# A graph attention layer pair: the edge counts as an added logarithm instead of a multiplication

## The chip, the cores and the metric

The kernel runs on one core of a Trainium2 chip. The metric is the device time of one execution in microseconds (us). The engines named below are TensorE (PE, with PEld for its weight loads), VectorE (DVE), ScalarE (ACT), GpSimd (POOL) and SyncE (SP, which issues most DMAs). Each engine works through its own queue in order; semaphores hold one back for another.

## The reference

Two graph attention layers over 512 nodes and 16,896 directed edges (8192 drawn pairs in both directions, and one loop per node), a residual and a layer norm. The first layer has 8 heads of 768 features, the second one head.

```python
def gat_layer(x, W, a_s, a_d, b, edge_index, concat):
    h = (x @ W).reshape(n, H, C)
    alpha_s = jnp.einsum('nhc,hc->nh', h, a_s)
    alpha_d = jnp.einsum('nhc,hc->nh', h, a_d)
    e = jax.nn.leaky_relu(alpha_s[src] + alpha_d[dst], NEG_SLOPE)
    m = jax.ops.segment_max(e, dst, num_segments=n)
    e = jnp.exp(e - m[dst])
    denom = jax.ops.segment_sum(e, dst, num_segments=n)
    alpha = e / (denom[dst] + EPS)
    msg = h[src] * alpha[:, :, None]
    out = jax.ops.segment_sum(msg, dst, num_segments=n)
    return out.reshape(n, H * C) + b
...
h = jax.nn.elu(gat_layer(x, W1, a_src1, a_dst1, b1, edge_index, concat=True))
x = _layernorm(x + gat_layer(h, W2, a_src2, a_dst2, b2, edge_index, concat=True))
```

An edge that occurs k times counts k times in the sum and in the denominator, and once in the maximum.

## The kernel before, in words

The edges are turned into a dense 512 by 512 matrix of counts, `cnt` (float32, four row blocks of 128 nodes, `[128, 4, 512]`), and a mask `absent` (bfloat16) that is 0 where there is an edge and 1e30 where there is none (`counted`, L490). Softmax is then done on dense rows. For a head h and a row block t:

- `lift` (L569, ACT) makes the negated logits of the block, 128 x 512, in a tile `q`;
- `leak` (L575, DVE) applies the leaky slope;
- `rank` (L578) adds the mask and takes the row minimum in one DVE instruction (L581, followed by a short read of the accumulator into `nmax`), and then ACT takes the exponential (L583);
- `weigh` (L788, DVE) multiplies by the counts and sums the row in one instruction (L791, followed by a read of the accumulator), adds a small constant (L794) and takes the reciprocal (L795);
- `turn_out` and `turn_in` (L809, L818) scale the block on ACT (L811), take it apart into halves of 16 bits (L814), transpose it by a DMA (L816), and put it back into `PT` (L819).

The whole order is written out by hand (`manual_schedule`); no scheduler moves anything. All products of matrices are of the Strassen kind: fewer products, more sums and differences on DVE, which are put between the matmuls as "fill". Head 0's first projection and the counting of edges come first (to about 60 us). Then, for each head h from 0 to 6, the loop at L991 has three stages:

- `mixed` (L869): the aggregation of head h, 256-column matmuls of L891, with the ELU on ACT and DVE;
- `second` (L442): this head's share of the second layer's projection, seven products P1, P2, P6, P7, P4, P5, P3, each for i = 0 and 1, matmuls of L364 with 384 columns. Their results are emptied from PSUM by ACT (L455) or DVE (L457, L459). **P4 is accumulated on the bank of P7, and P3 on that of P5**, after DVE has read the bank: so P4 waits for the emptying of P7. The loop at L1032 (n = 2 to 6) issues one product pair per step and puts between them, for head h + 1, `leak` and `rank` of block n - 2, `lift` of block n - 1, the emptying of the first half (`e0`), for n > 3 `weigh` and `turn_out` of block n - 4, and the emptying of the second half (`e1`);
- the projection of head h + 2 (`projection`, L382, or from head 3 on `by_thirds`, L407, matmuls of L423).

Head 0's own softmax runs earlier, with `rank` at L735 and `weigh` in `give` (L954), beside the counting and the projection of head 1. The second layer's aggregation and the layer norm (L1234 on) end the kernel.

In the trace each matmul of L364 stands as two instructions, so a step n of `second` (two products of three matmuls) has 12.

The program has a second copy of the whole pass, for edge lists that the first can't count; it is not run with these inputs. The lines that set the order in `second` are these:

```python
q = [lift(h + 1, 0)]
for n in range(2, 7):
    (m0, e0), (m1, e1) = pairs[2 * n:2 * n + 2]
    m0()
    if not last:
        m1()
    if n < 6:
        leak(q[n - 2])
        rank(q[n - 2], n - 2)
    if n < 5:
        q.append(lift(h + 1, n - 1))
    ...
    e0()
```

Of the kernel before, what the change touches and what calls it, by code (L numbers as in the profile page):

```python
# [8 lines left out]
F32 = mybir.dt.float32  # L9
# [4 lines left out]
AF = mybir.ActivationFunctionType  # L14
ALU = mybir.AluOpType
# [3 lines left out]
EPS_DEN = 1e-16  # L19
EPS_LN = 1e-5  # L20
NO_EDGE = -1e30


def kernel(tc: tile.TileContext, *args):
# [12 lines left out]
def gat_pass(  # L37
# [16 lines left out]
    nc = tc.nc  # L54
    P = 128
# [15 lines left out]
    const = ctx.enter_context(tc.tile_pool(name="const", bufs=1))  # L71
# [3 lines left out]
    small = ctx.enter_context(tc.tile_pool(name="small", bufs=4))  # L75
# [171 lines left out]
    for j in range(2):  # L247
        nc.vector.tensor_reduce(picks[:, j:j + 1], ident.rearrange("p (j k) -> p k j", k=32)[:, j, :], axis=AX.X,
                                op=ALU.add)
    far = const.tile([P, 1], F32, name="far")  # L250
    nc.vector.memset(far, -NO_EDGE)
    wide = keep.tile([P, 2, SQ], F32, name="wide")
    nc.vector.memset(wide, 0.0)

# [69 lines left out]
    cnt = keep.tile([P, NT, N], F32, name="cnt")  # L324
    absent = keep.tile([P, NT, N], BF16, name="absent")
# [243 lines left out]
    def lift(h, t):  # L569

        q = BC[h] if 0 < h < H and t + 1 == NT else qpool.tile([P, N], F32, name="q")
        nc.scalar.activation(q, BC[h][:, :N], AF.Identity, bias=AL[h][1][:, t:t + 1], scale=-1.0)
        return q
# [4 lines left out]
    def rank(q, t):  # L578

        nmax = small.tile([P, 1], F32, name="nmax")  # L580
        nc.vector.tensor_tensor_reduce(out=q, in0=q, in1=absent[:, t, :], scale=1.0, scalar=-NO_EDGE,  # L581
                                       op0=ALU.add, op1=ALU.min, accum_out=nmax)
        nc.scalar.activation(q, q, AF.Exp, bias=nmax, scale=-1.0)  # L583
        return q

    def turn_b1():
        psb = mm.tile([P, 512], F32, name="mm")
# [12 lines left out]
    if not general:  # L600
# [95 lines left out]
        for n, batch in enumerate(batches):  # L696
# [32 lines left out]
            if n + 1 == len(batches):  # L729
                spread(0)  # L730
                q = [lift(0, t) for t in range(NT)]
# [11 lines left out]
    else:  # L743
        for t in range(NT):
            ps = mm.tile([P, 512], F32, name="mm")
            for c in range(EC):
# [3 lines left out]
                                        op0=ALU.is_equal)  # L750
# [36 lines left out]

    def weigh(q, t, scale=True):  # L788

        den = small.tile([P, 1], F32, name="den")  # L790
        nc.vector.scalar_tensor_tensor(q, q, 1.0, cnt[:, t, :], op0=ALU.mult, op1=ALU.mult,  # L791
                                       accum_out=den)
        rden = small.tile([P, 1], F32, name="rden")
        nc.vector.tensor_scalar(rden, den, EPS_DEN, None, op0=ALU.add)  # L794
        nc.vector.reciprocal(rden, rden)  # L795
        if scale:
            nc.vector.tensor_scalar(q, q, rden, None, op0=ALU.mult)  # L797
        return rden
# [192 lines left out]
    for h in range(H - 1):  # L991
        if 0 < h < H - 2:
            B3, rest_of_thirds = load_thirds(h + 2)
        elif h:
            A[H] = []
            for j, a in ((2, a_src2[0]), (4, a_dst2[0])):
                v = wpool.tile([P, HK, HALF], F32, name=f"w2t{j}").rearrange("p k n -> p (k n)")[:, :D]
                nc.sync.dma_start(v, row_bcast(a))
                A[H].append(v)
            last_sum = load_w2(H - 1, "w2")  # L1000
        GA, gsums = left(gT, gS)
        halves = [half_logits(h + 1, t) for t in ((0, 1) if h else (0, 1, 3))]
        besides[2:2] = [s_ for s_, _ in halves] + [lambda: row_out(h + 1)]
        finish = mixed(h, AA, BB, besides + [d_ for _, d_ in halves] + behind)
        besides, behind = [], []
        if h == 0:
            load_w1(2)()
        if h + 2 < H:
            load_a(h + 2, a_src1[h + 2], a_dst1[h + 2])
            attend = attended(h)  # L1010
        pairs = second(h, GA, B2)
        for m, _ in pairs[:2]:
            m()
        pairs[0][1]()
        for f in finish:
            f()
        gsums[0]()
        pairs[1][1]()
        gsums[1]()
        if pending:  # L1020
            pending.pop(0)()
        pairs[2][0]()
        gsums[2]()
        pairs[3][0]()
        gsums[3]()
        if pending:
            pending.pop(0)()
        pairs[2][1]()
        pairs[3][1]()
        last = h + 2 == H  # L1030
        q = [lift(h + 1, 0)]
        for n in range(2, 7):  # L1032
            (m0, e0), (m1, e1) = pairs[2 * n:2 * n + 2]
# [4 lines that stand above are left out]
                leak(q[n - 2])  # L1038
                rank(q[n - 2], n - 2)
            if n < 5:  # L1040
                q.append(lift(h + 1, n - 1))
            if last:

                if n > 4:
                    turn_in(n - 5)
                if n == 6:
                    turn(q[2], 2)
                if n == 6:
                    weigh(q[3], 3)
                m1(lambda: turn(q[3], 3) if n == 6 else None)  # L1050
            if not last and n == 6:
                turn_in(0)
                turn_out(q[2], 2, weigh(q[2], 2, scale=False))
            e0()
            if last and 2 < n < 6:
                weigh(q[n - 3], n - 3)
                if n < 5:
                    turn_out(q[n - 3], n - 3)
            if not last and 3 < n < 6:
                turn_out(q[n - 4], n - 4, weigh(q[n - 4], n - 4, scale=False))  # L1060
            if not last and n == 6:
                turn_out(q[3], 3, weigh(q[3], 3, scale=False))
                if 0 < h:
                    sums = rest_of_thirds()
                    reload_x()
                load_w2(h + 1)()
            e1()
            for f in in_second[:1]:
                f()
            del in_second[:1]  # L1070
            if 0 < h and not last and 2 < n < 6:
                attend[n - 3]()
        if 0 < h and h + 2 < H:
            pairs = by_thirds(h + 2, XB, B3)
            AA, sums3 = left_sums(h + 1)
            B2, sums2 = right(W2[h + 1], "w1")
            for n in range(15):
                pairs[n][0]()
                for p in {0: ("P6", "P2"), 1: ("P4",), 4: ("P10",), 5: ("P0",), 6: ("P1",), 9: ("P7",),
                          12: ("P3",)}.get(n, ()):  # L1080
                    sums[p]()
                if n == 5:
                    BB, rsums_ = right_sums()
                    sums3 += rsums_
                if n in (2, 3, 5, 6, 8, 9, 10):
                    for _ in range(2 if n == 8 else 1):
                        sums3.pop(0)()
                if n in (11, 13):
                    logits(h + 2, HS[h + 2], 2 + (n - 11) // 2)
                if n in in_third:  # L1090
                    in_third.pop(n)()
                if n == 14:
                    sums2[0]()
                    behind = sums2[1:]
                pairs[n][1]()
                if n in (1, 2, 4):
                    turn_in((n + 2) // 2)
            assert not sums3
        elif h + 2 < H:
            B_, sums = right(W1[h + 2], "w2")  # L1100
            pairs = projection(h + 2, XA, B_)
            for n in range(14):
                pairs[n][0]()
                if n == 0:
                    for f in attend:
                        f()
                    B2, sums2 = right(W2[h + 1], "w1")
                if n in (1, 3):
                    sums[n // 2]()
                if n == 1:  # L1110
                    AA, sums3 = left_sums(h + 1)
                pairs[n][1]()
                if n in (1, 2, 4):
                    turn_in((n + 2) // 2)
                if n == 5:
                    BB, sums3 = right_sums()
                if 1 <= n < 9:
                    sums3.pop(0)()
                if n == 0:
                    XB, early, store, late_ = x_thirds()  # L1120
                if n in (2, 3, 5, 6, 7, 8, 9):
                    early.pop(0)()
                if n == 9:
                    store()
                if n in (10, 12):
                    logits(h + 2, HS[h + 2], 2 + (n - 10) // 2)
                if n == 13:
                    late_["P10"]()
                    behind = [sums2[0], late_["P8"]]
                    in_second, in_third = [sums2[1], late_["P13"], late_["P9"]], {2: late_["P12"], 7: late_["P5"]}  # L1130
        else:
            last_sum()
            B2, sums2 = right(W2[H - 1], "w1")
# [65 lines left out]
    q, rden = [lift(H, 0)], []  # L1199
# [96 lines left out]
```

## Time and profile before

| what | us |
| --- | --- |
| median of three runs (641.05 to 641.44) | 641.15 |
| the profiled execution's own time | 640.93 |
| its span, first to last instruction | 639.1 |
| PE busy | 628.2 |
| DVE busy | 525.8 |
| ACT busy | 305.9 |
| mean granted clock of TensorE | 0.998 |
| L791 on DVE, 36 times, without the reads of its accumulator | 24.6 |
| reads of that accumulator, 36 times | 3.0 |
| L583 on ACT, 36 times | 25.8 |
| table loads on ACT, 2 | 1.3 each |

"Busy" is the union of an engine's instructions. Matmuls overlap each other in the records, so a short stop between two of them does not show as idle time; it shows in the distance between their starts. The timeline gives starts and durations in us, neighbouring instructions of one kind in one row (x12: twelve of them), and in brackets how long the engine had been idle before, and for whom it waited.

### The profile page before, as it was taken

To read this page: it belongs to the slowest core of one execution; us is meant where nothing else is said; L and a number is where in the kernel's file an instruction comes from. 1 tells how busy PE (TensorE), PEld (TensorE's weight loads), DVE (VectorE), ACT (ScalarE), POOL (GpSimd) and SP (SyncE) were. 2 spreads that over 40 slices of the span, in tenths; PEclk is the share of its full clock that TensorE was granted. 3 is DMA by queue.
4 is the path that set the end of the run, shared out by engine and by line. 5 is a ranking of instruction groups with operands and counts; after the bars stand their busy time and mean duration, and the time that the engine had idled before them with its cause. 6 is when DMAs were issued, how large, how long until landed. Compare 5 with 4: busy or idle time off the path is not lost.

```text
span 639.1 us, 7665 instructions
## 1 busy us (share of the span) xinstructions
PE 628.2 (98%) x2509; PEld 435.4 (68%) x2509; DVE 525.8 (82%) x1138; ACT 305.9 (48%) x510; POOL 63.6 (10%) x105
## 2 busy tenths in 40 slices
PE   8999999999999999999999999999999999999995
PEld 5555586556756886588857886588857886645553
DVE  8989889897789878878788878878888878876775
ACT  5874745730718145551728145551728145543440
POOL 1300011010300220010300230010300110000000
PEclk9999999999999999999999999999999999999999
DMA  8993488696905987099925986198915991410122
GB/s 299 325 237 90 89 237 276 156 265 213 261 23 89 325 228 185 17 269 235 235 73 109 316 228 174 21 269 240 237 59 125 318 303 23 116 40 1 31 60 77
DMA packets 86844, 109.87 MB, mean 172 GB/s; under 512 B 40150, under 2 KB 67982, under 8 KB 86030
## 3 DMA queue, kind: packets, MB, share of 16 engines
q1 hardware_dynamic: 70590, 87.42, 42.6%
q0 software_dynamic: 15776, 21.30, 19.9%
q10 hardware_dynamic: 432, 0.59, 0.3%
q8 instruction: 22, 0.36, 0.2%
q14 instruction: 24, 0.20, 0.1%
HBM read 95.12 MB, written 2.90 MB: 153 GB/s over the span
## 4 chain that ended last, share of the span: by engine, by line
PE 94%; DVE 3%; DMA 1%; ACT 1%; issue 0%; SPq 0%; POOL 0%; DVEq 0%; POOLq 0%; ACTq 0%
PE mm L364 43%; PE mm L423 20%; PE mm L891 18%; PE mm L837 3%; PE mm L1242 3%; PE held L364 2%; PE tr L664 1%; DMA a_s<-in_L_gnn_a_src_dram 1%; PE held L544 1%; PE bc L664 0%; ACT os L636 0%; DVE offsets L309 0%; PE tr L1166 0%; DMA drow<-turned 0%; DVE h L459 0%
## 5 line engine op out<-in xcount | busy, mean ns | idle before, releaser
L364 PE MATMUL mm<-w,gT 128*128 128x384 f32 x252 | 83.6, 486 | 0.0
L583 ACT ACTIVATE q<-q,nmax 128x512 f32<-128x512 f32 x36 | 25.8, 721 | 92.4 <-DVE nmax L581 92.4
L364 PEld LDWEIGHTS mm<-w,gT 128*128 128x128 f32 x252 | 47.9, 190 | 31.9
L891 PE MATMUL mm<-PT,hs 128*128 128x256 f32 x252 | 61.3, 379 | 0.0
L364 PE MATMUL mm<-w1t,gS 128*128 128x384 f32 x180 | 60.6, 487 | 0.0
L429 ACT ACTIVATE hs<-mm 128x512 f32<-128x512 f32 x30 | 17.9, 596 | 87.0 <-PE mm L423 72.4
L891 PEld LDWEIGHTS mm<-PT,hs 128*128 128x128 f32 x252 | 47.8, 190 | 7.3 <-issue 0.4
L364 PEld LDWEIGHTS mm<-w1t,gS 128*128 128x128 f32 x180 | 34.1, 190 | 24.0 <-DVE w1t L356 0.5
L431 DVE TENSOR_TENSOR hs<-hs,mm 128x512 f32<-128x512 f32 x45 | 30.8, 685 | 23.0 <-PE mm L423 21.8
L459 DVE TENSOR_TENSOR h<-h,mm 128x384 f32<-128x384 f32 x72 | 38.9, 547 | 12.6 <-PE mm L364 12.3
L891 PE MATMUL mm<-pS,gS 128*128 128x256 f32 x168 | 43.2, 380 | 0.0
L819 ACT COPY PT<-zr 128x1024 uint16<-128x1024 uint16 x34 | 39.3, 1156 | 2.6 <-DMA zr<-pS 1.9
L423 PE MATMUL mm<-w2r,xT 128*128 128x256 f32 x160 | 37.9, 380 | 0.0
L423 PE MATMUL mm<-w2r,gT 128*128 128x256 f32 x160 | 37.5, 382 | 0.0
L891 PEld LDWEIGHTS mm<-pS,gS 128*128 128x128 f32 x168 | 31.8, 190 | 4.7 <-DVE pS L864 0.4
L423 PEld LDWEIGHTS mm<-w2r,xT 128*128 128x128 f32 x160 | 30.3, 190 | 5.4 <-DVE hs L431 0.2
L423 PEld LDWEIGHTS mm<-w2r,gT 128*128 128x128 f32 x160 | 30.0, 190 | 5.8 <-DVE hs L431 1.9
L364 PE MATMUL mm<-w1t,gT 128*128 128x384 f32 x96 | 32.4, 487 | 0.0
L895 ACT COPY u<-mm 128x256 f32<-128x256 f32 x21 | 7.8, 372 | 48.7 <-PE mm L891 48.7
L638 DVE TENSOR_SCALAR os<-nodes,idx 128x512 bf16<-128x512 f16 x104 | 29.5, 358 | 1.4 <-PE tr L664 1.4
L814 ACT COPY pS<-q 128x1024 uint16<-128x1024 uint16 x26 | 27.1, 1044 | 4.2 <-DVE q L797 3.6
L364 PE MATMUL mm<-w,gS 128*128 128x384 f32 x84 | 28.7, 487 | 0.4 <-DVE h L459 0.4
(233 smaller groups left out, 1264.8 us busy)
## 6 DMA issues: line engine op xcount, KB each, us to landing
w2r<-in_L_gnn_W_dram SPq DMA_DIRECT2D x48, 384.0 KB, 10.3
w<-in_L_gnn_W_dram SPq DMA_DIRECT2D x43, 384.0 KB, 10.6
gT<-xd SPq DMA_DIRECT2D x5, 1280.0 KB
w1t<-in_L_gnn_W_dram SPq DMA_DIRECT2D x9, 576.0 KB
w<-in_L_gnn_W_dram POOLq DMA_DIRECT2D x8, 576.0 KB, 8.5
w1t<-in_L_gnn_W_dram POOLq DMA_DIRECT2D x7, 576.0 KB, 9.6
w2t<-in_L_gnn_W_dram SPq DMA_DIRECT2D x15, 256.0 KB, 6.9
w2t<-in_L_gnn_W_dram POOLq DMA_DIRECT2D x15, 256.0 KB, 8.9
```

Of the source, the lines that this page charges most:

```text
L364: nc.tensor.matmul(ps[:, :HALF], A_[p][:, k, i * P:(i + 1) * P], B_[p][:, k, :], start=start and k == 0, stop=k == HK - 1, skip_group_chec ...
L423: nc.tensor.matmul(bank[chain][:, i * TH:(i + 1) * TH], A_[p][:, k, i * P:(i + 1) * P], B_[p][:, k, :], start=first and i == k == 0, stop= ...
L429: nc.scalar.activation(out(o), ps, AF.Copy, scale=how)
L431: nc.vector.tensor_tensor(out(o), out(o), ps, op=how)
L459: nc.vector.tensor_tensor(a, a, ps, op=ALU.subtract if p == "P7" else ALU.add)
L583: nc.scalar.activation(q, q, AF.Exp, bias=nmax, scale=-1.0)
L638: nc.vector.tensor_scalar(o, nodes, idx[:, c:c + 1], None, op0=ALU.is_equal)
L814: nc.scalar.copy(apart.rearrange("p (h n) -> p h n", h=2), q.bitcast(U16).rearrange("p (n h) -> p h n", h=2))
L819: nc.scalar.copy(PT.rearrange("p s n -> p (s n)").bitcast(U16).rearrange("p (s n h) -> p s n h", s=NT, h=2)[:, :, t * P:(t + 1) * P, :], p ...
L837: nc.tensor.matmul(ps[:, :N], HS[h][:, s, c * P:(c + 1) * P], PT[:, s, :], start=(s == 0), stop=(s == NT - 1))
L891: nc.tensor.matmul(bank[p][:, :HN], A_[p][:, k, c * P:(c + 1) * P], B_[p][:, k, :], start=over is None and k == 0, stop=k == 1, skip_group ...
L1242: nc.tensor.matmul(ps[:, :cols.stop - cols.start], PT[:, s, t * P:(t + 1) * P], h2[:, s, cols], start=(s == 2), stop=(s == 1))
```

## The change

After head 0's softmax, the logarithm of all counts (plus 1e-18) is taken once, in place, by one ACT instruction over 128 x 2048 (`logarithms`), and the mask minus that logarithm replaces the counts, one row block at a time, on DVE (`fold_count`). From head 1 on, and in the second layer, `rank` adds this instead of `absent`, the row sums come out of ACT's exponential, and `weigh` keeps only the small constant and the reciprocal. Head 0 keeps the multiplication on VectorE. The row minimum now is that of the logits with the logarithm added. In the built program the order of PE, POOL and SP is the same instruction by instruction; on ACT one table load stands ahead of the logarithm and another ahead of the next exponential.

```diff
+TINY = 1e-18
...
+    tiny = const.tile([P, 1], F32, name="tiny")
+    nc.vector.memset(tiny, TINY)
...
     def rank(q, t):
 
         nmax = small.tile([P, 1], F32, name="nmax")
-        nc.vector.tensor_tensor_reduce(out=q, in0=q, in1=absent[:, t, :], scale=1.0, scalar=-NO_EDGE,
-                                       op0=ALU.add, op1=ALU.min, accum_out=nmax)
-        nc.scalar.activation(q, q, AF.Exp, bias=nmax, scale=-1.0)
+        nc.vector.tensor_tensor_reduce(out=q, in0=q, in1=(cnt if folded else absent)[:, t, :], scale=1.0,
+                                       scalar=-NO_EDGE / 2 if folded else -NO_EDGE, op0=ALU.add, op1=ALU.min, accum_out=nmax)
+        if folded:
+            dens[t] = small.tile([P, 1], F32, name="den")
+            nc.scalar.activation(q, q, AF.Exp, bias=nmax, scale=-1.0, accum_out=dens[t])
+        else:
+            nc.scalar.activation(q, q, AF.Exp, bias=nmax, scale=-1.0)
         return q
+
+    folded, dens = [], {}
+
+    def logarithms():
+        nc.scalar.activation(cnt, cnt, AF.Ln, bias=tiny)
+        folded.append(True)
+
+    def fold_count(t):
+
+        nc.vector.tensor_tensor(cnt[:, t, :], absent[:, t, :], cnt[:, t, :], op=ALU.subtract)
...
     def weigh(q, t, scale=True):
 
-        den = small.tile([P, 1], F32, name="den")
-        nc.vector.scalar_tensor_tensor(q, q, 1.0, cnt[:, t, :], op0=ALU.mult, op1=ALU.mult,
-                                       accum_out=den)
+        if folded:
+            den = dens.pop(t)
+        else:
+            den = small.tile([P, 1], F32, name="den")
+            nc.vector.scalar_tensor_tensor(q, q, 1.0, cnt[:, t, :], op0=ALU.mult, op1=ALU.mult,
+                                           accum_out=den)
...
         pairs[2][1]()
         pairs[3][1]()
         last = h + 2 == H
+        if h == 0:
+            logarithms()
+            fold_count(0)
         q = [lift(h + 1, 0)]
         for n in range(2, 7):
...
                 leak(q[n - 2])
                 rank(q[n - 2], n - 2)
             if n < 5:
+                if h == 0:
+                    fold_count(n - 1)
                 q.append(lift(h + 1, n - 1))
```

## The prediction, made before the changed kernel ran

> **What bounds the kernel now.** I read the page first, its busy line and its shares of the chain of work that ended last.
>
> ```profile
> PE 628.2 (98%) x2509; PEld 435.4 (68%) x2509; DVE 525.8 (82%) x1138; ACT 305.9 (48%) x510; POOL 63.6 (10%) x105
> ...
> PE 94%; DVE 3%; DMA 1%; ACT 1%; issue 0%; SPq 0%; POOL 0%; DVEq 0%; POOLq 0%; ACTq 0%
> ```
>
> PE is busy for 98% of the span and carries 94% of the chain. DVE at 82% is the engine that the change relieves, and it carries 3%. So an average says nothing yet: the question is at which places PE stops for DVE. The view of who waited for whom, for weight loads from 100 to 600 us (they stand ahead of their matmuls and so show a wait first), gives these (us in total, times, longest):
>
> ```profile
> PEld mm L891 <- DVE zr L905: 3.1, 7, 0.8
> PEld mm L423 <- DVE hs L431: 2.2, 6, 0.4
> ...
> PEld mm L364 <- DVE h L459: 1.5, 2, 1.0
> ...
> PEld mm L364 <- DVE h L457: 0.2, 1, 0.2
> ```
>
> L905 belongs to the aggregation and L431 to the projections: no softmax work of L576 to L797 stands between the matmuls there. In `second`, where the removed instruction (L791) stands for heads 1 to 6, PE waited for DVE at L459 twice only, and at L457 once. I then read the timeline around these three. First head 0's `second`, where the change adds its work:
>
> ```profile
> 107.30 0.48 ACT L455 COPY h<-mm 128x384 f32<-128x384 f32 x1 [1.46 <-PE mm L364]
> ...
> 109.98 0.69 DVE L576 SCALAR_TENSOR_TENSOR q<-q 128x512 f32<-128x512 f32 x1
> ...
> 111.08 4.03 PE L364 MATMUL mm<-w,gT 128*128 128x384 f32 x12
> 111.31 1.01 DVE L459 TENSOR_TENSOR u<-u,mm 128x384 f32<-128x384 f32 x2
> ...
> 114.14 0.55 DVE L457 TENSOR_SCALAR h<-mm 128x384 f32<-128x384 f32 x1
> ...
> 114.75 3.62 PEld L364 LDWEIGHTS mm<-w1t,gT 128*128 128x128 f32 x12 [0.25 <-DVE h L457]
> 114.95 4.03 PE L364 MATMUL mm<-w1t,gT 128*128 128x384 f32 x12
> ...
> 118.82 4.03 PE L364 MATMUL mm<-w1t,gS 128*128 128x384 f32 x12
> ```
>
> The reader is to see the rhythm: steps of 12 matmuls begin 3.87 us apart (111.08, 114.95, 118.82), which is 12 x 0.322, so PE loses nothing here. But P4 (at 114.95) needs P7's bank emptied, and that (L457) ended at 114.69: its weight load already waited 0.25. DVE has about 0.2 us to spare at this point and no more.
>
> Second, head 1's `second`, the one place where the removed multiplication is on the path:
>
> ```profile
> 192.11 0.69 DVE L791 SCALAR_TENSOR_TENSOR q<-q,cnt 128x512 f32<-128x512 f32 x1
> 192.14 4.03 PE L364 MATMUL mm<-w1t,gS 128*128 128x384 f32 x12
> ...
> 195.97 0.55 DVE L459 TENSOR_TENSOR h<-h,mm 128x384 f32<-128x384 f32 x1
> ...
> 196.58 3.52 PEld L364 LDWEIGHTS mm<-w,gS 128*128 128x128 f32 x12 [1.02 <-DVE h L459]
> ```
>
> P3 should have begun at 192.14 + 3.87 = 196.01 and began at 196.58: 0.57 late, for the emptying that began at 195.97. DVE runs without a pause from 188.35 to there, extra sums of the x blocks and L985 among it, and L791 is one link. For heads 2 to 5 the same steps show no wait.
>
> **The change part by part.**
>
> *Removed:* L791 for 32 of its 36 times. 32 x (0.685 + 0.082 for the read of its accumulator) = 24.5 us of DVE. Of this only the link at 192.11 is on the path. Without it (next independent DVE instruction 0.73 earlier) the emptying that starts at 195.97 starts at about 195.3 and ends at 195.8, just ahead of 196.01. Gain: the 0.57, and 0.10 that a restarted PE loses in its first pair (in rows of after a stop the second matmul starts 0.43 after the first instead of 0.32): at most 0.67. A weight load would like its data 0.2 earlier than its matmul, so a part may stay; I take **0.6**, with 0.4 and 0.7 as ends. The other 31 stand beside PE work that doesn't wait for them, and are worth nothing. The other late emptying, at 188.16, has no L791 ahead of it and stays. The row sums in the last head (L797 to the transposes on PE, 556 to 559 us) look like a chain, but the wait there at 559.81 is for the copy of `PT` on ACT behind PE's own transposes, which stand between the last matmuls; nothing is gained.
>
> *Added on ACT, ahead of head 1's first `lift`:* a table load, the logarithm, and a second load before the next exponential. What a load costs, and what 512 against 256 columns cost:
>
> ```profile
> L1254 ACT ACT_TABLE_LOAD x1 | 1.3, 1283 | 0.0
> ...
> L829 ACT ACTIVATE zr<-zr,b1T 128x512 f32<-128x512 f32 x21 | 15.2, 722 | 0.7
> L829 ACT ACTIVATE u<-u,b1T 128x256 f32<-128x256 f32 x21 | 10.7, 509 | 0.7
> ```
>
> No row has 2048 columns. From these two, (722 - 509) / 256 = 0.83 ns a column, so 0.72 + 1536 x 0.83 ns = 2.0 us (an estimate from these rows; the copies L814, 1.04 us for 1024 of 16 bits, would make it 1.9 to 2.1). In order: the copy ends at 107.78; load 107.80 to 109.08; logarithm to 111.1; `lift` (0.71) to 111.7, where before it had ended at 108.4. The second load, 111.73 to 113.0, falls into ACT's wait for `nmax` (113.15 by the next part) and costs nothing; that a load runs ahead of the wait of its function is shown by the one for the square root, at 613.10, five us before it.
>
> *Added on DVE:* four folds of 128 x 512, 0.69 each (row L581, which also mixes float32 with bfloat16; 0.61 from start to start). The first waits for the logarithm, and DVE's queue is in order: behind it stand `leak`, `rank` and both emptyings of P6 and P7. Fold 0 starts at 111.13, `leak` at 111.74 instead of 109.98: 1.76 late. Fold 1 stands ahead of P6's emptyings (+0.61; P6's banks are not wanted soon, five banks are in use), fold 2 ahead of P7's (+0.61). Before, DVE had idled 0.47 between P6's emptying and the second `leak`; that cushion is used up: 1.76 + 0.61 - 0.47 + 0.61 = 2.5 us, so L457 begins at 116.6 and ends at 117.2. P4 then starts at 117.2 instead of 114.95, and loses 0.1 for the restart: **2.4 us of PE idle**. Who waits behind it: nothing else. P5 has fresh banks; its emptying comes at about 123.3 to 123.9, and P3 wants it at 125.1. Fold 3 lies in a DVE wait for P4. The four folds are paid once, and everything behind P4 in PE's order moves by the whole 2.4, since PE shows no later pause that an early DVE or DMA could give back, other than those counted.
>
> *Row sums on ACT:* no accumulator read on ACT is in this trace. The nearest rows are DVE's (82 ns) and the shortest ACT instruction (L500, 166 ns); below nothing is excluded, since the exponential itself stays. I take 0.08, and 0 to 0.17 as ends. It delays only the second `lift` of head 1 on the path, where DVE is ready at the same time: 0 to 0.15, inside the 2.4. Elsewhere `lift` ends over 2 us before its `leak` (184.0 against 186.2).
>
> *The constant:* one more memset of 128 x 1 on DVE ahead of the first long copy (L309) in the start-up chain; its neighbours start 0.01 to 0.02 apart and last 0.06: +0.03.
>
> *Sum:* 2.4 - 0.6 + 0.03 = +1.8 on the profiled execution, 640.93 to 642.8. The median of the runs is 0.22 above that execution, so **643.0** there.
>
> **The one rule that speaks against more than this.** A load's row is 1.28, and nothing in this trace follows a load at once: after the first (ending at 3.0) ACT waits for PE until 4.88, after the second until 618.55. A pause behind a load would be hidden in both. The Trainium skill, "ScalarE: Activation LUTs", section "What ACT_TABLE_LOAD costs", puts a drain of about 1.38 us on top of the 1.28, 2.66 us for each switch; no run here shows it so far. By that figure P4 would stop for about 1.4 us more for the first load and 1.1 more for the second, an estimate of 645.5.
>
> **The rivals.**
>
> 1. *A pause behind each table load.* The place is the same; the logarithm and the first exponential begin later. By rows the pause is 0 to 1.87 (the idle time behind the first load). The first one delays P4 in full, the second less 0.2 of slack on ACT: up to 1.87 + 1.67 = 3.5 more, 643.0 to 646.5, and 644.8 in the middle. For it: nothing in the rows excludes it. Against it: the load's own row starts 0.02 after the instruction before it ended.
>
> 2. *The delay is given back.* At 165.0 and 171.7 PE waits for DVE (L905; the wait at 171.7 is 0.77, the longest one), and in the chain of waits this stretch stands with DMA pieces. If DVE, relieved, or the transfers, 2.4 us earlier against PE, close both, some 0.9 comes back: 642.1, within 0.2% (1.28 us, about what a measurement of this kernel can tell from no change). Against it: DVE works without a pause into 171.23, with a 1.35 us weight sum (L356) that the change leaves.
>
> 3. *Faster: DVE's queue is late everywhere.* If the waits at L905 and L431 were a backlog that the 24.5 us of DVE work leaves behind, their 3.1 + 2.2 = 5.3 us would go too: 643.0 - 5.3 = 637.7. It decides once over 3.2 of the 5.3 come back (the 1.85 of the forecast and 1.28). Against it: DVE itself idles for PE shortly before them (0.28, 0.30 and 0.42 ahead of L431 between 214 and 220 us), so it had caught up, and the waits are made by the DVE instructions placed just there.
>
> **How the numbers follow.** The forecast, one stop of about 2.4 in head 0's `second` and 0.6 regained in head 1's: 0.63. Rival 1: 0.19. Rival 2: 0.13. Rival 3: 0.05. The forecast's own bounds (logarithm 1.9 to 2.1, accumulator read, 0.4 to 0.7 regained) make 642.6 to 643.5. For the range I go down to rival 2 and up to a pause of 1.4 behind both loads: 641.9 to 645.5. Slower by over 0.2%: the forecast nearly whole and rival 1, 0.80. Within: rival 2 and a rest of the forecast, 0.15. Faster: 0.05.
>
> **What would show it.** In the changed profile: two loads of 1.28 and one logarithm of about 2.0 on ACT at 108 to 113; a PE wait of over 2 us for DVE at L457 (its new line) near 115, and none like it in other heads; a fold that waits for ACT; P3 of head 1 at 3.87 behind P5; DVE's busy time lower by 24.5 - 2.8 = some 21.7 us, with PE's pauses elsewhere as before. The forecast is wrong if P4 doesn't wait, if ACT stands still between load and logarithm, or if the waits at L905 and L431 shrink.

## The result, and the profile after

| | median us | lowest to highest | executions |
| --- | --- | --- | --- |
| before | 641.21 | 640.90 to 641.78 | 8 |
| changed | 643.82 | 642.59 to 644.40 | 8 |

The ratio is 1.0035, 95% interval 1.0024 to 1.0046: slower by 2.6 us. The changed kernel's times fall into two groups, 642.59 to 642.75 (three executions, mean granted clock 0.998) and 643.69 to 644.40 (five, 0.995 or 0.996). The profiled one is of the second group: 644.22, span 642.4.

The page of the changed kernel, the lines that answer to the two shown of before:

```profile
PE 629.8 (98%) x2509; PEld 436.9 (68%) x2509; DVE 507.3 (79%) x1079; ACT 313.0 (49%) x545; POOL 63.6 (10%) x105
...
PE 94%; DVE 2%; ACT 1%; DMA 1%; issue 0%; SPq 0%; DVEq 0%; ACTq 0%
```

DVE is relieved of 18.5 us, its share of the chain falls from 3% to 2%, and the time grows all the same. Who waited for whom, weight loads from 100 to 600 us (the lines of `second` are now L460 for before's L457, L462 for L459; L925 is before's L905, L434 before's L431):

```profile
PEld mm L911 <- DVE zr L925: 3.1, 7, 0.8
PEld mm L367 <- DVE h L460: 2.7, 1, 2.7
PEld mm L426 <- DVE hs L434: 1.9, 5, 0.4
...
PEld mm L367 <- DVE h L462: 0.5, 1, 0.5
```

One new wait of 2.7, and one wait at L462 gone (1.5 in two, now 0.5 in one). The 3.1 at the aggregation is as before; at the projections 1.9 in five stands for 2.2 in six. The timeline of head 0's `second`:

```profile
107.61 1.28 ACT L596 ACT_TABLE_LOAD   x1
...
108.90 2.00 ACT L596 ACTIVATE cnt<-cnt,tiny 128x2048 f32<-128x2048 f32 x1
...
110.93 0.69 DVE L601 TENSOR_TENSOR cnt<-absent,cnt 128x512 f32<-128x512 bf16 x1 [1.07 <-ACT cnt L596]
111.53 1.28 ACT L588 ACT_TABLE_LOAD   x1
111.55 0.69 DVE L579 SCALAR_TENSOR_TENSOR q<-q 128x512 f32<-128x512 f32 x1
...
112.89 0.69 DVE L601 TENSOR_TENSOR cnt<-absent,cnt 128x512 f32<-128x512 bf16 x1
113.01 0.72 ACT L588 ACTIVATE q<-q,nmax 128x512 f32<-128x512 f32 x1 [0.19 <-DVE nmax L584]
...
113.64 0.19 ACT L588 ACTIVATION_READ_ACCUMULATOR q<-q,nmax 128x1 f32 x1
...
115.81 0.69 DVE L601 TENSOR_TENSOR cnt<-absent,cnt 128x512 f32<-128x512 bf16 x1
...
116.42 1.01 DVE L460 TENSOR_SCALAR h<-mm 128x384 f32<-128x384 f32 x2
...
117.02 5.83 PE L367 MATMUL mm<-w1t,gT 128*128 128x384 f32 x12 [2.09 <-DVE h L460]
```

The chain can be read downwards: the table load, the logarithm, fold 0, `leak`, fold 1, fold 2, the emptying of P7 (L460), P4. P4 begins at 117.02. Then comes what the prediction did not have: its 12 matmuls take 5.83 us, where before they took 4.03. The view by stretches shows why (columns: stretch, length, busy time and count for PE, PEld, DVE, ACT, POOL, then the granted clock of TensorE, DMA share, GB/s):

```profile
114.80:117.00 2.20, 0.12 (x1) 0.00 (x0) 2.17 (x6) 1.07 (x3) 0.00 (x0) 1.00 1.12 261
117.00:118.00 1.00, 0.98 (x3) 0.68 (x4) 1.00 (x2) 0.35 (x1) 0.00 (x0) 1.00 1.15 247
118.00:119.00 1.00, 1.00 (x3) 0.53 (x2) 0.97 (x4) 0.15 (x1) 0.00 (x0) 0.62 0.90 200
119.00:120.00 1.00, 1.00 (x3) 0.49 (x2) 0.42 (x1) 1.00 (x3) 0.00 (x0) 0.50 0.13 31
...
122.00:123.00 1.00, 1.00 (x4) 0.57 (x3) 0.11 (x1) 0.74 (x1) 0.00 (x0) 1.00 0.00 0
```

Over a microsecond after PE has resumed, the granted clock drops to one half, and it is whole again by 122; in the trace's clock records from 118.25 to 121.66, for 3.41 us. PE is busy throughout these slices (1.00), so it isn't waiting: its matmuls are slower. And the gain, in head 1's `second`:

```profile
196.00 4.03 PE L367 MATMUL mm<-w1t,gS 128*128 128x384 f32 x12
...
199.87 2.42 PE L367 MATMUL mm<-w,gS 128*128 128x384 f32 x7
```

P3 follows P5 by 3.87 where it was 4.44.

The starts of PE's steps, put side by side from the traces of all kernels of this study, account for nearly the whole difference (us; "head 1" is P5 to the projection behind P3; all stretches between the columns agree to 0.02):

| kernel | start to P6 | P7 to P4 | P4 to P5 | head 1 | projection to last matmul | end |
| --- | --- | --- | --- | --- | --- | --- |
| before | 107.11 | 3.87 | 3.87 | 8.41 | 431.72 | 6.85 |
| changed | 106.92 | 6.13 | 5.67 | 7.74 | 431.62 | 7.05 |
| e1, removal alone | 107.14 | 3.87 | 3.87 | 7.74 | 431.63 | 6.83 |
| e2, addition alone | 107.44 | 6.09 | 3.97 | 8.41 | 431.64 | 6.86 |
| e3, PE kept busy | 106.61 | 6.13 | 3.97 | 7.74 | 431.63 | 7.17 |
| e4, logarithm later | 106.96 | 3.87 | 3.87 | 7.74 | 431.64 | 6.85 |
| e5, no table switch | 106.68 | 4.96 | 3.97 | 7.74 | 431.64 | 6.84 |
| e6, pass doubled | 107.00 | 8.17 | 6.99 | 7.74 | 431.62 | 7.19 |
| e7, folds behind | 106.91 | 5.53 | 3.97 | 7.74 | 431.63 | 6.85 |
| e8, changed again | 106.61 | 6.13 | 5.67 | 7.74 | 431.64 | 6.85 |

Changed against before: +2.26 (the stop), +0.10 (the restart), +1.70 (the half clock), -0.67 (head 1), -0.10 behind it, -0.19 and +0.20 at both ends: +3.3, the difference of the two spans. The first column scatters by 0.8 among programs that are alike up to there but for one memset, and the last by 0.36; so a comparison of a few tenths is read from the middle columns, not from single times.

Most of the scatter in the first column has a cause that the clock records show. The clock is whole for the first time between 4.41 and 6.72 us, and in eight of the ten traces P6 starts the later, the later that is (4.41 and 106.61 in e8, 5.61 and 106.92 in the change, 6.72 and 107.44 in e2). In the other two, before and e4, PE also waits 0.40 for DVE near 81 us; why only there stays open. So the -0.19 ahead of P6 is not put down to the change.

### The profile page after: what moved, and what is told of

Same layout as the page of the kernel before. It is cut to its first block, busy times and chain, and to the rows that moved or that the text cites. A ratio compares the mean times of both kernels' runs of the same rounds, so it can differ in the third digit from the quotient of the medians.

```text
span 642.4 us, 7641 instructions
## 1 busy us (share of the span) xinstructions
PE 629.8 (98%) x2509; PEld 436.9 (68%) x2509; DVE 507.3 (79%) x1079; ACT 313.0 (49%) x545; POOL 63.6 (10%) x105
## 4 chain that ended last, share of the span: by engine, by line
PE 94%; DVE 2%; ACT 1%; DMA 1%; issue 0%; SPq 0%; DVEq 0%; ACTq 0%
PE mm L367 43%; PE mm L426 20%; PE mm L911 18%; PE mm L857 3%; PE mm L1267 3%; PE held L367 2%; PE tr L681 1%; DMA q<-drow 1%; PE bc L234 1%; PE held L547 1%; PE bc L681 0%; ACT os L653 0%; PE mm L265 0%; ACT cnt L596 0%; PE tr L1191 0%
## 5 line engine op out<-in xcount | busy, mean ns | idle before, releaser
L588 ACT ACTIVATE q<-q,nmax 128x512 f32<-128x512 f32 x32 | 23.1, 722 | 88.5 <-DVE nmax L584 88.5
L462 DVE TENSOR_TENSOR h<-h,mm 128x384 f32<-128x384 f32 x72 | 39.2, 551 | 31.1 <-PE mm L367 30.6
L434 DVE TENSOR_TENSOR hs<-hs,mm 128x512 f32<-128x512 f32 x45 | 30.8, 684 | 23.0 <-PE mm L426 23.0
L367 PE MATMUL mm<-w1t,gT 128*128 128x384 f32 x96 | 34.2, 508 | 2.1 <-DVE h L460 2.1
L367 PEld LDWEIGHTS mm<-w1t,gT 128*128 128x128 f32 x96 | 18.8, 198 | 16.3 <-DVE h L460 2.7
```

Of the source, the lines that this page charges most:

```text
L367: nc.tensor.matmul(ps[:, :HALF], A_[p][:, k, i * P:(i + 1) * P], B_[p][:, k, :], start=start and k == 0, stop=k == HK - 1, skip_group_chec ...
L434: nc.vector.tensor_tensor(out(o), out(o), ps, op=how)
L462: nc.vector.tensor_tensor(a, a, ps, op=ALU.subtract if p == "P7" else ALU.add)
L588: nc.scalar.activation(q, q, AF.Exp, bias=nmax, scale=-1.0, accum_out=dens[t])
```

## The experiments

The theory: the change costs one stop of PE at P4 of head 0, made of the first load, the logarithm and the folds in DVE's queue; it gains 0.67 in head 1; and a pause of that length lets TensorE's clock fall in some executions, which adds some 1.1 to 1.7. The rivals: the row sums on ACT cost something by themselves; the two groups of times have another cause; a table switch or the folds cost wherever they stand.

### e1: the removal alone

```diff
-            logarithms()
-            fold_count(0)
+            folded.append(True)
...
-        in1=(cnt if folded else absent)[:, t, :]
+        in1=absent[:, t, :]
...
-                if h == 0:
-                    fold_count(n - 1)
```

> The removal alone: rows sums by ScalarE's exponential from head 1 on, no logarithm, no folds, the mask without counts (so from head 1 on a repeated edge counts once; that part of the computation is left out). Theory: the multiplication was on the path at one place only, so 641.2 - 0.7 = 640.5, P3 of head 1 begins 3.87 us behind P5, P4 of head 0 doesn't wait, clock 0.998 in every execution. Rival (the 32 accumulator reads of 0.19 us on ScalarE cost something by themselves): 641.2 or above.

Measured: 640.15 against 641.32 of before on the same chip, ratio 0.9982 (0.9973 to 0.9991). P4 doesn't wait, head 1's stretch is 0.67 shorter, all else is alike (table). So the 32 accumulator reads on ACT, 0.186 each, cost nothing, and 24.5 us less of DVE's instructions are worth one stop of 0.67. The medians differ by 1.2, with an interval from 0.6 to 1.7 in which the 0.67 lies; no stretch behind P6 shows more.

### e2: the addition alone

```diff
+    def logarithms():
+        nc.scalar.activation(PT, cnt, AF.Ln, bias=tiny)
+
+    def fold_count(t):
+        nc.vector.tensor_tensor(PT[:, t, :], absent[:, t, :], PT[:, t, :], op=ALU.subtract)
```

> The addition alone: the kernel before, with the two loads, the logarithm and the four folds at the places of the change, written into a tile that is dead there (PT) and not used; the loads after the logarithm, the multiplications and row sums stay as before. Theory: P4 of head 0 waits as in the change, +2.4 without a fall of the clock (643.6) and +4.1 with it (645.3), both kinds among the executions, and P3 of head 1 is as late as before (0.57). Rival (the stop belongs to the new data path, not to the wait for the logarithm): 641.2.

Measured: 643.59, ratio 1.0038 (1.0025 to 1.0052); four executions from 643.47 to 643.71 at 0.997 and one of 644.35 at a mean clock of 0.995. The profiled one is of the four. The fifth has the lower clock that a fall gives, but it lies 0.8 above the four and not the 1.7 that was expected; no trace of it was kept, so what it paid is open. Its P4, and its P3 of head 1:

```profile
117.50 4.14 PE L367 MATMUL mm<-w1t,gT 128*128 128x384 f32 x12 [2.05 <-DVE h L460]
...
199.24 4.14 PE L367 MATMUL mm<-w,gS 128*128 128x384 f32 x12 [0.41 <-DVE h L462]
```

The same stop as in the change, without its other half; P3 is as late as before, because the multiplication is still there. The two halves of the change add up: nothing of the stop belongs to the new data path. And here a pause of 2.05 was not followed by the half clock (the row of P4 takes 4.14).

### e3: PE kept busy while it waits

```diff
+            if h == 0 and n == 4:
+                hot_ = bc.tile([P, 512], F32, name="bc")
+                for _ in range(9):
+                    nc.tensor.matmul(hot_, blank[:, :P], blank, start=True, stop=True)
             m0()
```

> The changed kernel with 9 bf16 matmuls of 512 columns on zeros ahead of P4 (9 x 0.216 = 1.9 us), in the time in which TensorE waits. Theory (the pause itself halves the clock behind it): no fall of the clock in any execution, 642.6 in all, spread below 0.6 us. Rival (the executions of 643.7 to 644.4 have another cause, such as the transfers or the phase at the start): the same mixture of 642.6 and 644.0 as the change, or slower by the work added.

Measured: 642.44 (642.10 to 643.13 in eleven executions), ratio 1.0020 (1.0011 to 1.0029).

```profile
114.46 2.11 PE L1062 MATMUL bc<-blank 128*128 128x512 bf16 x9
...
116.72 4.14 PE L367 MATMUL mm<-w1t,gT 128*128 128x384 f32 x12 [0.16 <-DVE h L460]
```

P4 starts as late as in the change (6.13 behind P7), but no execution reaches the upper group, and P4 takes 4.14. So the upper group is made by PE's own pause: with useless work in it, the pause costs its length and no more. The profiled execution makes a close pair with that of e8, the change run again: the clock was whole for the first time at 4.42 in one and 4.41 in the other, P7 and P4 start within 0.01 of each other, and the clock fell at 117.05 in e8, and in e3 not before 635.89, behind the last matmul. The spread came to 1.0 instead of under 0.6; the first column of the table scatters by 0.8.

### e4: the logarithm where nobody waits

```diff
-        if h == 0:
-            logarithms()
-            fold_count(0)
...
+        nc.scalar.activation(small.tile([P, 1], F32, name="again"), tiny, AF.Exp)
...
+                if n == 5:
+                    logarithms()
+                if n in (9, 11):
+                    fold_count((n - 9) // 2)
...
+            if h == 1 and n == 2:
+                fold_count(2)
+                fold_count(3)
```

> The change with the logarithm moved behind head 1's multiplications, into the projection of head 2 where ScalarE stands still for 18 us, with a small exponential behind it that takes the second load there; two folds where VectorE idles in that projection (0.78 and 0.84 us), two between the emptyings of P6 in head 1's second stage (1.38 us idle). Head 1 multiplies by counts too. Theory: nothing waits for the logarithm, P3 of head 1 still gains, 640.5, clock 0.998 throughout. Rival (a table switch or the folds cost wherever they stand): above 641.2.

Measured: 640.38 (640.02 to 640.91), ratio to before 0.9986 (0.9977 to 0.9995): the one version with the whole computation that beats both, by 0.9 against before and by over 3 against the change.

```profile
135.92 1.28 ACT L596 ACT_TABLE_LOAD   x1
...
137.21 2.00 ACT L596 ACTIVATE cnt<-cnt,tiny 128x2048 f32<-128x2048 f32 x1
...
139.23 1.28 ACT L597 ACT_TABLE_LOAD   x1
...
140.53 0.20 ACT L597 ACTIVATE again<-tiny 128x1 f32<-128x1 f32 x1
```

The same two loads, the same logarithm and the same four folds, worth 2.4 to 4.1 us in the change, cost nothing here, since ACT has no other work and DVE had idle time for each fold. The stretch from P3 of head 0 to the end is e1's.

### e5: the pass without a table switch

```diff
-        nc.scalar.activation(cnt, cnt, AF.Ln, bias=tiny)
+        nc.scalar.activation(cnt, cnt, AF.Identity, bias=tiny)
```

> The changed kernel with the identity in place of the logarithm (so the counts enter as they are and not as logarithms; the work is the same 128 x 2048 pass, but no table is switched). Theory: the first load was in the chain and the second was not; the pass ends at 109.7, just ahead of VectorE's being free at 110.05, so the first leak is 0.7 late instead of 1.76, and P4 stops for 1.3 instead of 2.4: 641.9; a pause of 1.2 leaves the clock at full speed in every execution. Rival (more than the load's own 1.28 hangs on a switch): below 641.5.

Measured: 641.20, ratio 1.0001 (0.9992 to 1.0010); every execution at a clock of 0.997 or more.

```profile
115.61 4.14 PE L367 MATMUL mm<-w1t,gT 128*128 128x384 f32 x12 [0.93 <-DVE h L460]
```

P4 is 1.09 late (expected 1.2 and 0.1 for the restart), so the first load had been worth 2.26 - 1.09 = 1.17, within its own 1.28. The time came out under the 641.9 that was expected, and under the 641.5 that the rival named; the stretches explain 0.1 of that, and in the profiled execution 0.43 lies ahead of P6, where this program is like the others. By the stretches from P7 on it should be 0.4 slower than before, which the interval (-0.5 to +0.6) contains. So the rival, time that hangs on a switch beyond the load, falls by the stop, not by the total.

### e6: the pass doubled

```diff
         nc.scalar.activation(cnt, cnt, AF.Ln, bias=tiny)
+        nc.scalar.activation(cnt, cnt, AF.Identity, bias=tiny)
```

> The changed kernel with a second pass over the counts behind the logarithm, an identity of the same size (2.0 us; it adds the 1e-18 once more, which alters nothing in the result). Theory: P4 stops for 2.4 + 1.9 = 4.3, and a pause that long halves the clock in every execution, at 1.1 to 1.7 each: 646.0 to 646.6, all of one kind. Rival (the fall of the clock doesn't depend on the length of the pause): the mixture of two kinds, 644.9 and 646.4.

Measured: 646.91 (646.27 to 647.88), ratio 1.0086 (1.0072 to 1.0100); all five at a clock of 0.993 to 0.995, none in a lower group.

```profile
119.15 7.16 PE L367 MATMUL mm<-w1t,gT 128*128 128x384 f32 x12 [4.14 <-DVE h L460]
```

The stop grew by 2.04; the second pass lasts 2.00. The clock was half for 6.83 us (118.44 to 125.27 in the clock records), twice as long as in the change, so P4 to P5 took 6.99 instead of 3.97: 3.0 us for the clock, more than the 1.1 to 1.7 that was expected of it, and the median lies 0.3 above the 646.6 that was the expectation's upper end.

### e7: the folds behind the emptyings

```diff
-            if n < 5:
-                if h == 0:
-                    fold_count(n - 1)
...
             e1()
+            if h == 0 and n < 5:
+                fold_count(n - 1)
```

> The changed kernel with the folds of blocks 1 to 3 behind both emptyings of their step instead of ahead. Theory: of the 2.4 the fold of block 2 stood ahead of P7's emptying, 0.61; the fold of block 1 is ahead of it either way. P4 stops for 1.75, 642.0 without a fall of the clock; with a pause of 1.65 the clock falls less often than in the change, if at all. Rival (only the logarithm's wait counts, the folds lie in VectorE's idle time): 642.6 to 644, as the change.

Measured: 641.71, ratio 1.0010 (1.0001 to 1.0019); eleven executions from 641.39 to 642.66 at 0.997 or 0.998.

```profile
116.41 4.14 PE L367 MATMUL mm<-w1t,gT 128*128 128x384 f32 x12 [1.49 <-DVE h L460]
```

P7 to P4 is 5.53 instead of 6.13: one fold, 0.60, as worked out. A pause of 1.49 brought no half clock in the profiled execution, and by the mean clocks in none of the others.

### e8: the change once more

> The changed kernel once more, beside the others on one chip. Theory: two kinds of executions, 642.6 with the clock at 0.998 and 643.7 to 644.4 with it at 0.996 or less, split by whether the clock falls behind the pause at 115 to 117. Rival (the two kinds belonged to the chip of the first runs): one kind.

Measured: 643.69 (642.57 to 643.91), ratio 1.0035 (1.0022 to 1.0049); four executions in the upper group at 0.995 or 0.996, one at 642.57 and 0.997. The profiled one is of the upper group, with the clock at half from 117.05 to 120.46. Two groups again, in another set of executions; whether the first set ran on the same chip is not on record.

## Why the prediction was right, and where it fell short

It was right in direction, in place and within its range, and the terms that it gave a size can be checked one by one:

- **The stop.** Predicted 2.4 at P4 of head 0, with L457 (now L460) beginning at 116.6 and P4 at 117.2. Measured 2.26 and 0.10 for the restart; 116.42 and 117.02. The links: logarithm 2.0 by slope, 2.002 in the trace; load 1.28; fold 0.69. Without the loads (e5) the stop shrinks by 1.17, with one fold moved out of the way (e7) by 0.60.
- **The second load is hidden.** It ran from 111.53 to 112.81, ahead of an exponential that waited for DVE until 113.01.
- **The gain.** Predicted 0.6, measured 0.67, by e1 without any of the addition.
- **What is worth nothing.** The other 31 multiplications: shown by e1, where no other stretch shortened by more than 0.1.
- **The row sums' read.** The term was undersized: 0.08, with 0.17 as the upper end, against 0.187. It cost nothing that the stretches show (e1).
- **The memset.** Its +0.03 can't be told from the scatter of 0.8 ahead of P6.
- **DVE's busy time** fell by 18.5 and not by 21.7. Busy time is a union, and neighbouring rows overlap by about 0.08 each, so instructions taken singly add up to more than their union.

Rival 1, a pause behind each load, is refuted: the logarithm starts 0.01 after its load ended (108.89 and 108.90), and in e4 the small exponential starts 0.02 after the second (140.51 and 140.53). The Trainium skill, "ScalarE: Activation LUTs", section "What ACT_TABLE_LOAD costs", counts a drain of 1.38 on top of the load's 1.28; the load's own length agrees with these rows, the drain does not show. Rival 2, the delay given back at 165 to 172, didn't happen: the wait there is 0.77 before and after, 3.9 us later. Rival 3 fell with the waits at L905 and L431: 3.1 and 2.2 before, 3.1 and 1.9 after; the 1.9 also stands in e2, where nothing is taken off DVE.

**The step that fell short** is "loses 0.1 for the restart", the whole price that was put on PE's pause. In both profiled executions of the change the pause was also followed by 3.41 us at half clock, which cost 1.70 us. Seven more of the thirteen executions (five of eight and four of five in all) lie in the same upper group and have the lower mean clock; that their clock fell at the same place is inferred from this, since no trace of them was kept. That is why the median lies 0.8 above the forecast of 643.0, and above the 643.5 that ended the forecast's own bounds, while the executions of the lower group lie 0.2 to 0.4 below. The range reached far enough for another reason than this, the pause behind the loads, which did not occur: that the median still lies in it is luck.

The clock's rule can be read in part from the records. The times at full clock between start, fall and end are 112.64 in the change, e6 and e8, and 628.05 or 631.47 in those where the clock fell only at the end of the kernel: 33, 184 and 185 times 3.413, the length of the fall. So the clock seems to be set in windows of 3.413, whose phase differs from execution to execution. Laid over the pauses: in the change the window from 114.84 to 118.25 held all of the 2.09 of idle time (61%), in e8 the one from 113.64 to 117.05 too, and the clock fell at their ends. In e2 a border (115.94) cut the pause in two, with some 1.6 (46%) in the second window, and it didn't fall; in e7 a whole pause of 1.49 (44%) lay in one window and it didn't either. Laid over the rest of the ten traces in the same way, wherever the clock was whole, the windows agree: none with up to 47% of idle time (e6, near the end) is followed by a fall, and all from 61% on are (65% and 68% at the end of e3 and e1). A threshold between 47% and 61% of a window fits all of these, an estimate from these traces; that it is a share of a window, and not the longest unbroken pause in it, was not tried. For coming back the clock asked for more: in e6 PE was idle for 0.70 of the first window at half clock (21%) and the clock stayed at half for another one, while in the change and e8 PE worked through that window and the clock came back at its end. The Trainium skill, "TensorE: Matmul & The Clock Gate", section "What's actually happening", has such a free-running window of 3413 ns, and these records agree with it; its section "HAM oscillation — how this bites in real kernels" gives as a rule that pauses of over about 3.4 us are to be avoided, and here 2.09 was enough.

## What to carry to other kernels

Work taken off an engine that is busy for 82% of the span was worth one stop of 0.67 us, because the bound engine waited for it at one place; look for the places, not for the sum. A one-time step that other instructions queue behind belongs where its engine stands still and the next user is far off: the same loads, logarithm and folds cost 2.4 to 4.1 us in front of `leak` and nothing 28 us later. Where TensorE is the bound, a pause of about 2 us must be counted with the clock that may fall behind it (1.70 us here), and useless matmuls in the pause kept it up here (nine in e3).

## What the runs showed of the hardware that was not expected

- A pause of TensorE of 2.09 us was followed by 3.41 us at half clock in both profiled executions, and by times and mean clocks in nine of thirteen; one of 4.14 by 6.83 us in its profile, and with a lower mean clock in all five executions; pauses of 1.49 and 0.93 in neither profile, and by the mean clocks in none of eleven each.
- ACT's accumulator read is an instruction of its own, 0.187 us, against 0.082 on DVE.
- Switches of ACT's table cost 1.28 us and nothing behind it, in three places (the next instruction started 0.01 to 0.02 after the load).
- Programs alike up to 107 us reached that point between 106.61 and 107.44 in their profiled executions, in eight of ten in the order in which their clock had first become whole (4.41 to 6.72 us).
